# A cleared spare tile behind some gathers, and eleven row buffers for layer 1, in a two-layer graph network on Trainium2

## The chip, the cores and the metric

The kernel runs on one core of a Trainium2 chip. The metric is the device time of one execution in microseconds; the median of several executions counts. TensorE is PE in the profile (PEld is its weight load), VectorE is DVE, ScalarE is ACT, GpSimd is POOL, and SyncE (SP) issues most plain transfers. GpSimd issues all gathers, which are indirect DMA instructions: 128 row numbers go in, and 128 rows of a table in DRAM come out, one row to a partition.

## The reference

12,500 nodes with 128 features each and 200,000 edges, sorted by their destination. Everything is float32. Cut to what matters:

```python
h0 = maximum(layernorm(x), 0)
deg, wsum = segment_sum(1, dst), segment_sum(w, dst)
w = w / maximum(wsum, 1e-12)[dst]
feat = relu(h0 @ W_pool + b_pool)
neigh = segment_max(feat[src] * w, dst)          # layer 1: max over edges, 0 where deg is 0
rst = h0 @ W1_self + neigh @ W1_neigh + b1
h = relu(rst / maximum(norm(rst), 1e-12))
neigh2 = segment_sum(h[src] * w, dst) / maximum(deg, 1)   # layer 2: sum over edges
out = x + relu(h @ W2_self + neigh2 @ W2_neigh + b2)
```

Each layer fetches one row for every edge (`feat[src]`, `h[src]`), which is a gather of 200,000 rows of 512 bytes. That is done in groups.

## The kernel before, in words

**Groups.** The edges stand in 391 groups of 512 (the last has 320). A group's rows are fetched by four gathers of 128 rows, all issued by GpSimd in `gather` (L508, the instruction at L513). The nodes stand in 25 groups of four tiles of 128.

**Preparation.** The node groups are read, normalized and multiplied by W_pool: DVE takes the statistics, ACT makes the normalized tile (L622), PE transposes it (L624), ACT copies it out of PSUM (L645), PE multiplies it by W_pool (L647 for the bias, then L649, four matmuls that the trace shows as eight), and DVE or ACT clips the product at zero (`clip`, L608 for DVE), which goes to a table `feat_d` in DRAM. Background work on the edges (weights, degrees, flags) runs beside it on all engines. The table is complete only at the end of this stage. So that GpSimd isn't idle meanwhile, the first 17 edge groups (FIRST) gather rows of x itself, 68 gathers (called at L666); layer 1 normalizes and multiplies those edges' rows by W_pool itself (lines L527 to L557). GpSimd is kept in step with the preparation in its first part by a clear of a single column (L626), which waits for ACT.

**Layer 1.** Groups 17 to 390 gather rows of `feat_d` (called at L945). The consumer of a group is a pipeline over several steps: PE transposes the rows (L964), DVE multiplies by the weights (L1006), scans along the edges for a running maximum per destination (L979), picks and copies (L990, L999, L1002), PE transposes back (L1019), ACT copies (`rows`, L974), PE puts the rows at their nodes (L1028), and ACT adds that window to the layer's result (L914). Node groups whose edges are done are normalized and go to a table `h_d`.

**Layer 2.** Three early groups, and then groups 3 to 390, gather rows of `h_d` (called at L1127). DVE makes a matrix of places and weights (L1063, L1068), PE multiplies (L1075), and DVE adds the window (L1080). Node quads then make the output.

**Row buffers.** `buffer(g, wide)` says where group g's rows go. In layer 1 there is a ring of 18 buffers at first, then one of 14, and from group 113 on one of 4 (DEEP): memory that was lent is then in use for other things. The pool of full buffers itself has 11 tiles (RING + MORE). Layer 2 uses 4. The first gather of a group waits until PE has read what its buffer held; every gather also waits for the DMA of the gather eight before it. So the size of the ring is how many groups GpSimd can run ahead of the consumer.

**Order.** It is written out by hand in both layers and the preparation (manual schedules): each engine takes its instructions in the order of the code, and waits at the first whose inputs are not there.

Of the kernel before, what the change touches and what calls it, by code (L numbers as in the profile page):

```python
# [7 lines left out]
F32 = mybir.dt.float32  # L8
# [5 lines left out]
OP = mybir.AluOpType  # L14
# [4 lines left out]
P = 128  # L19
D = 128  # L20
# [16 lines left out]
LESS = 3 * WIDE  # L37
MID = 14
LEAST = LESS + 4 * MID
# [5 lines left out]
SCRATCH = 8192  # L45
MORE = 3
DEEP = 4


@with_exitstack  # L50
def gnn_kernel(ctx, tc, x, src, dst, ew, w_pool, b_pool, w1s, w1n, b1, w2s, w2n, b2, out):
# [13 lines left out]
    nc = tc.nc  # L65
# [6 lines left out]
    NG = GF + 1  # L72
# [4 lines left out]
    const = ctx.enter_context(tc.tile_pool(name="const", bufs=1))  # L77
    dram = ctx.enter_context(tc.tile_pool(name="dram", bufs=1, space=DRAM))

    feat_d = dram.tile([NP, D], F32, name="feat_d")  # L80
    h_d = dram.tile([NP, D], F32, name="h_d")
# [13 lines left out]
    bases = const.tile([1, NT * P], I32)  # L95
    unfit = const.tile([1, 1], I32)
    W = {name: const.tile([P, D], F32, name=f"w_{name}") for name in ("pool", "1s", "1n", "2s", "2n")}
    bp_all, b1_all, b2_all = (const.tile([P, D], F32, name=f"b_{i}") for i in range(3))
    ident = const.tile([P, P], F32)
    cols = const.tile([P, 2, LW], F32)  # L100

    both = ExitStack()
# [30 lines left out]
    def buffer(g, wide):  # L133
        if not wide:
            return full[g % DEEP]
        if WIDE <= g < WIDE + 3:
            k = g - WIDE
            return (work(f"f{k}").rearrange("p (q d) -> p q d", d=D) if k < 2 else ewT[:, 1])
        h = g if g < WIDE else g - 3
        if h < LESS:  # L140
            return ring[h % WIDE]
        return mid[(h - LESS) % MID] if h < LEAST else full[(h - LEAST) % DEEP]


    dr = rp.tile([P, NT, G + 2], I32)
# [63 lines left out]
    def load_rest():  # L209
# [11 lines left out]
        for t in range(1, NT):  # L221
# [3 lines left out]
            load_edges(nc.sync, ew, er, 0, t)  # L225


    diff = wk.tile([P, P], F32, bufs=1)
    nc.gpsimd.iota(diff, pattern=[[1, P]], base=0, channel_multiplier=-1,
                   allow_small_or_imprecise_dtypes=True)  # L230
    nc.gpsimd.iota(cols[:, 0, :], pattern=[[1, LW]], base=0, channel_multiplier=0,
                   allow_small_or_imprecise_dtypes=True)
# [3 lines left out]
    nc.gpsimd.iota(need, pattern=[[P, NT]], base=-LAG, channel_multiplier=1,  # L236
                   allow_small_or_imprecise_dtypes=True)
    nc.gpsimd.memset(agg1[:, NP:], 0.0)
    nc.vector.tensor_scalar(ident, diff, 0.0, None, op0=OP.is_equal)
    shift = {}  # L240
    for name, at in (("up", 1), ("up_wrap", 1 - P), ("down", -1), ("down_wrap", P - 1)):
        shift[name] = rp.tile([P, P], F32, name=f"shift_{name}")
        nc.vector.tensor_scalar(shift[name], diff, float(at), None, op0=OP.is_equal)
    nc.vector.tensor_scalar(need, need, RHO, None, op0=OP.mult)
    late_nodes = rp.tile([P, LATE], F32)
    nc.gpsimd.iota(late_nodes, pattern=[[P, LATE]], base=(HI - LATE) * P, channel_multiplier=1,
# [258 lines left out]
        ne = G if g < GF else TAIL  # L505
        return *divmod(g, P), ne, [(j, min(P, ne - j * P)) for j in range(-(-ne // P))]

    def gather(gt, table_d, g, only=None, last=None):  # L508

        t, r, ne, chunks = edges_of(g)  # L510
        limit = {} if last is None else dict(bounds_check=last, oob_is_err=False)
        for j, k in chunks if only is None else chunks[only:only + 1]:
            nc.gpsimd.indirect_dma_start(  # L513
                out=gt[:k, j, :], out_offset=None, in_=table_d[:, :],
                in_offset=bass.IndirectOffsetOnAxis(ap=srcT[:k, t, j, r:r + 1], axis=0), **limit)
        return gt


    gts = {}
# [43 lines left out]
    rest = load_rest()  # L563
# [47 lines left out]
    for i in range(len(groups) + 3):  # L611
# [50 lines left out]
        while raw_chunks and 1 <= i <= 17:  # L662
            r, j = raw_chunks[0]
            if r >= WIDE - NT and i < 15 or r > WIDE - 3 and i < 17 or i < 9 and len(raw_chunks) <= Q * FIRST - 3 * i:
                break
            gts[r] = gather(buffer(r, True), x, r, only=j)  # L666
            raw_chunks.pop(0)
        if i == len(groups) - 1:
            w_first, kt_first = (rp.tile([P, G], F32, name=f"r_f{k}") for k in range(2))
# [201 lines left out]
    with tc.manual_schedule(), tc.tile_pool(name="ew", bufs=3) as wk, \  # L871
# [61 lines left out]
        for i in range(max(turn) + 6):  # L933
# [8 lines left out]
            if i % KEPT == 0 and i and i + 2 < NG:  # L942
                keep_rows(i + 2, keep_tile())
            if FIRST <= i < NG:
                gts[i] = gather(buffer(i, True), feat_d, i)  # L945

            if i + 1 < NG:
                weight_rows(i + 1, wk.tile([P, G], F32, name="gs", bufs=2))
# [95 lines left out]
        i = NG  # L1044
# [5 lines left out]
    with tc.manual_schedule(), tc.tile_pool(name="ew2", bufs=3) as wk, \  # L1050
# [73 lines left out]
        first_groups = early_groups()  # L1124
        for i in range(max(turn) + 2):
            if EARLY <= i < NG:
                gts[i] = gather(buffer(i, False), h_d, i)  # L1127
                places(i)
            if EARLY <= i < NG:
                weighted(i)  # L1130
            if i + 4 in turn:
                n = turn[i + 4]
                if n % wide2(n) == 0:
                    xr = x_rows(wk, n, wide2(n), 2)
                xrs[n] = xr
            if late is not None:
                stages(late)
                late = None
            quad_stage(1)
            quad_stage(3)  # L1140
            if i in turn:
                n, xr = turn[i], xrs.pop(turn[i])
                if wide2(n) < Q:
                    late = nodes2(wk, ps, n, 1, strided(agg2, n, 1), xr)
                    next(late)
                elif n % Q == 0:
                    st = quad2(wk, pn, n, xr)
                    next(st)
                    for k in (1, 2, 3):
                        quads[i + k, k] = st  # L1150
            g = i - 1
            if EARLY <= g < NG:
                window_product(g)
            quad_stage(2)
            if i >= EARLY and i % 2:
                next(first_groups, None)
            if i == NG - 1:
                for n in (HI - 2, HI - 1):
                    own[n] = flip[:, 0] if n % 2 else ps.tile([P, Q, D], F32, name="pl", bufs=1)[:, 0]
                    linear_own(own[n], n, "2s")  # L1160
            g = i - 2
            if EARLY <= g < NG:
                window_add(g, window_at(mybir.EngineType.DVE, g))
# [122 lines left out]
```

## Time and profile before

| what | us |
|---|---|
| median of three runs | 4587.56 |
| the three runs | 4581.83, 4587.56, 4592.94 |
| the profiled execution, its own time | 4582.98 |
| its span, first to last instruction | 4581.2 |
| busy: POOL / PE / DVE / PEld / ACT | 2963.4 / 1950.3 / 1759.1 / 1623.2 / 422.1 |
| first and last gather of x | 10.60 and 110.91 |
| first and last gather of feat_d | 162.66 and 2347.16 |
| first and last gather of h_d | 2357.17 and 4568.24 |

The gathers' times are their starts on GpSimd. The span differs from the execution's own time by 1.8 us of start and end. In a row of a timeline, the number in brackets is the idle time of that engine before the instruction, with what ended it: another instruction, "issue" (nothing that the profile shows), or "remote" (in the chain of waits: "another core or an unknown queue"), a release whose origin the trace does not hold. In a row of windows stand the window, its length, and for each engine the busy time with the count of instructions, then the granted clock of PE, the share of the DMA engines and GB/s; where the view is limited to one line, only the engines that run that line have a column.

### The profile page before, as it was taken

Reading aid. Unit: us, or ns where it says so; the run is one execution under the profiler, and the core shown is the slowest. Engines: PE = TensorE matmul, PEld = TensorE weight load, DVE = VectorE, ACT = ScalarE, POOL = GpSimd, SP = SyncE. Lnnn points to the kernel's source line nnn. Section 1 sums busy time; section 2 is a strip of 40 time slices with the busy share of each in tenths; the row PEclk is TensorE's granted clock in tenths of the full one; section 3 lists DMA queues with packets and bytes.
Section 4 is the critical chain, followed back from the end, with each engine's and each line's share of the span. In section 5 each row is a group of like instructions: output and inputs, shape, how many; then the busy total and the mean of one; then the engine's idle time right before and its main releaser. Section 6 shows DMA issues by size and latency. Waiting matters only on the chain.

```text
span 4581.2 us, 30093 instructions
## 1 busy us (share of the span) xinstructions
PE 1950.3 (43%) x8086; PEld 1623.2 (35%) x8086; DVE 1759.1 (38%) x4405; ACT 422.1 (9%) x1257; POOL 2963.4 (65%) x3143
## 2 busy tenths in 40 slices
PE   3554444444344444443444443333333333333333
PEld 2443334333333333332344433333333333333333
DVE  3676667666666666665561111111111111111111
ACT  3531111111111111111110000000000000000000
POOL 5366664666666666666666666666666666666665
PEclk7765555555555555555555555555555555555555
DMA  4344444444444444443431122211121112112111
GB/s 134 107 117 122 127 120 117 117 119 120 117 119 117 117 120 118 118 121 113 120 96 48 46 57 55 54 51 51 50 56 51 51 51 55 52 51 56 51 51 51
DMA packets 193262, 396.94 MB, mean 87 GB/s; under 512 B 60623, under 2 KB 63822, under 8 KB 193088
## 3 DMA queue, kind: packets, MB, share of 16 engines
q0 software_dynamic: 100032, 204.97, 17.3%
q1 hardware_dynamic: 92320, 189.06, 13.6%
q8 instruction: 69, 1.13, 0.1%
q10 hardware_dynamic: 736, 0.92, 0.1%
q14 instruction: 105, 0.86, 0.1%
HBM read 374.96 MB, written 19.77 MB: 86 GB/s over the span
## 4 chain that ended last, share of the span: by engine, by line
POOL 29%; issue 26%; another core or an unknown queue 19%; DVE 13%; PE 11%; ACT 2%; DMA 1%; POOLq 0%; ACTq 0%; DVEq 0%
POOL gt L513 28%; DVE pm L979 4%; PE pm L964 3%; PE pn L1028 2%; DVE pm L1006 2%; PE two_pr L1019 2%; DVE sc L999 1%; DVE sq L816 1%; DVE sc L1002 1%; DMA gt<-h_d,srcT 1%; PE pa L1075 1%; PE pf L649 1%; ACT rows L974 1%; DVE sel L990 0%
## 5 line engine op out<-in xcount | busy, mean ns | idle before, releaser
L513 POOL DMA_INDIRECT gt<-h_d,srcT x1551 | 1467.7, 946 | 728.9 <-issue 414.2
L513 POOL DMA_INDIRECT gt<-feat_d,srcT x1303 | 1234.9, 948 | 671.8 <-issue 360.7
L1075 PE MATMUL pa<-s,gt 128*128 128x24 f32 x3102 | 716.7, 383 | 1260.4 <-DMA gt<-h_d,srcT 803.5
L1075 PEld LDWEIGHTS pa<-s,gt 128*128 128x128 f32 x3102 | 687.4, 325 | 1328.0 <-issue 813.2
L1080 DVE TENSOR_TENSOR way<-pa,way 128x41 f32 x391 | 77.7, 199 | 1726.2 <-remote 1016.0
L1019 PE MATMUL two_pr<-ident,sc 128*128 128x128 f32 x782 | 243.9, 412 | 942.4 <-ACT rows L974 557.2
L1006 DVE TENSOR_TENSOR pm<-pm,gs 128x512 f32<-128x512 f32 x390 | 271.8, 697 | 680.7 <-remote 428.4
L979 DVE TENSOR_TENSOR_SCAN pm<-kt,pm 128x512 f32<-128x512 bf16 x389 | 499.0, 1283 | 7.1
L1019 PEld LDWEIGHTS two_pr<-ident,sc 128*128 128x128 f32 x782 | 124.9, 201 | 1055.3 <-ACT rows L974 596.0
L964 PE MATMUL pm<-ident,gt 128*128 128x128 f32 x1303 | 323.8, 397 | 99.5 <-issue 54.3
L1028 PEld LDWEIGHTS pn<-sel,rows 128*128 128x128 f32 x1564 | 350.2, 308 | 0.2
L1028 PE MATMUL pn<-sel,rows 128*128 128x48 f32 x1564 | 334.7, 359 | 0.0
L964 PEld LDWEIGHTS pm<-ident,gt 128*128 128x128 f32 x1303 | 243.0, 222 | 135.3 <-issue 87.8
L974 ACT ACTIVATE rows<-two_pr 128x256 f32<-128x256 f32 x392 | 150.4, 384 | 1515.1 <-remote 1046.2
L990 DVE TENSOR_SCALAR sel<-cols,lastT,invT 128x48 f32<-128x48 f32 x782 | 253.4, 324 | 0.0
L832 ACT ACTIVATE oT<-pn,b_col 128x512 f32<-128x512 f32 x24 | 16.5, 689 | 2181.5 <-PE pn L797 701.8
L999 DVE COPY sc<-pm 128x256 f32<-128x256 f32 x391 | 165.8, 424 | 78.8 <-remote 67.3
L1002 DVE COPY_PREDICATED sc<-kt,pm 128x256 f32<-128x256 int16 x389 | 169.3, 435 | 3.9 <-remote 3.9
L513 POOL DMA_INDIRECT w2T<-feat_d,srcT x100 | 94.7, 947 | 97.8 <-DVE raw_mv L527 50.8
L1068 DVE TENSOR_TENSOR s<-place,w2T 128x96 f32<-128x96 f32 x391 | 100.8, 258 | 74.9 <-remote 35.0
L1063 DVE TENSOR_TENSOR place<-place,locT 128x96 f32<-128x96 f32 x391 | 100.9, 258 | 0.3 <-DVE way L1080 0.3
L914 ACT ACTIVATE way<-pn 128x48 f32 x391 | 81.8, 209 | 120.8 <-issue 46.9
(288 smaller groups left out, 1622.8 us busy)
## 6 DMA issues: line engine op xcount, KB each, us to landing
gs<-in_edge_weight SPq DMA_DIRECT2D x389, 256.0 KB
kt<-keep_d SPq DMA_DIRECT2D x97, 512.0 KB
gt<-h_d,srcT POOLq DMA_INDIRECT x1551
gt<-feat_d,srcT POOLq DMA_INDIRECT x1303
feat_d<-fr SPq DMA_DIRECT2D x24, 256.0 KB
xr<-in_x SPq DMA_DIRECT2D x24, 256.0 KB
out<-o SPq DMA_DIRECT2D x24, 256.0 KB
h_d<-sq SPq DMA_DIRECT2D x23, 256.0 KB
```

The lines of the kernel that those rows point to most:

```text
L513: nc.gpsimd.indirect_dma_start(out=gt[:k, j, :], out_offset=None, in_=table_d[:, :], in_offset=bass.IndirectOffsetOnAxis(ap=srcT[:k, t, j, ...
L964: nc.tensor.transpose(pms[i][:, j * P:j * P + k], gt[:k, j, :], ident[:k, :k])
L974: nc.scalar.activation(rws[g][:k, j, :], pr[:k, j, :], AF.Copy)
L979: nc.vector.tensor_tensor_scan(pm[:, :ne], kt[:, :ne], pm[:, :ne], carry, op0=OP.add, op1=OP.max)
L990: nc.vector.tensor_scalar(part, cols[:k, 1, :], lastT[:k, t, j, r:r + 1], invT[:k, t, j, r:r + 1], op0=OP.is_equal, op1=OP.mult)
L999: nc.vector.tensor_copy(sc[:, :ne // 2], two[:, :, 1])
L1002: nc.vector.copy_predicated(sc[:, :ne // 2], new[:, :, 1], two[:, :, 0])
L1006: nc.vector.tensor_tensor(pms[i][:, :n], rows[:, :n], ws.pop(i)[:, :n], OP.mult)
L1019: nc.tensor.transpose(prs[g][:k, j, :], sc[:, j * P:j * P + k], ident)
L1028: nc.tensor.matmul(pas[g], rows[:k, j, :], sel[:k, j, :], start=j == 0, stop=j == len(chunks) - 1)
L1063: nc.vector.tensor_tensor(hit, iota, locT[:, t, :, r:r + 1].to_broadcast([P, Q, PART]), OP.is_equal)
L1075: nc.tensor.matmul(pas[g][:, PART_AT[j]:PART_AT[j] + PART], gt[:k, j, :], s[:k, j, :], start=j == len(chunks) - 1, stop=j == 0, skip_group ...
```

## The change

Four things:

- `gather` has a new argument `rest`. With it, each gather instruction is followed on GpSimd by a `memset` of a tile `spare`, 128 partitions by 256 float32 columns, which nothing reads afterwards. It is set for the gathers of x except group 0's (64 instructions), for layer 1's groups up to 63 that gather `feat_d` (17 to 63, 188 instructions), for layer 1's last 26 groups (103) and layer 2's last 8 (31): 386 in all.
- In layer 1 the last ring has eleven buffers and not four; layer 2 keeps four.
- `spare` takes the memory of the bias row `bp_all`, which is read at the very start. The first clear waits for DVE to have read it; each further clear waits only for the clear before.
- To make room, the identity and the four shifted identities are slices of one 128x384 tile, made by one comparison in place of five.

```diff
+REST = 256
+REST_TO = 64
+REST_FROM = 26
+REST_END = 8
...
-    bp_all, b1_all, b2_all = (const.tile([P, D], F32, name=f"b_{i}") for i in range(3))
-    ident = const.tile([P, P], F32)
+    b1_all, b2_all = (const.tile([P, D], F32, name=f"b_{i}") for i in range(2))
+    spare = const.tile([P, REST], F32)
+    bp_all = spare[:, :D]
+    near_ones = const.tile([P, 3 * P], F32)
+    ident = near_ones[:, P:2 * P]
...
-        return mid[(h - LESS) % MID] if h < LEAST else full[(h - LEAST) % DEEP]
+        return mid[(h - LESS) % MID] if h < LEAST else full[(h - LEAST) % len(full)]
...
-    diff = wk.tile([P, P], F32, bufs=1)
-    nc.gpsimd.iota(diff, pattern=[[1, P]], base=0, channel_multiplier=-1,
+    diff = wk.tile([P, 3 * P], F32, bufs=1)
+    nc.gpsimd.iota(diff, pattern=[[1, 3 * P]], base=-P, channel_multiplier=-1,
...
-    nc.vector.tensor_scalar(ident, diff, 0.0, None, op0=OP.is_equal)
-    shift = {}
-    for name, at in (("up", 1), ("up_wrap", 1 - P), ("down", -1), ("down_wrap", P - 1)):
-        shift[name] = rp.tile([P, P], F32, name=f"shift_{name}")
-        nc.vector.tensor_scalar(shift[name], diff, float(at), None, op0=OP.is_equal)
+    nc.vector.tensor_scalar(near_ones, diff, 0.0, None, op0=OP.is_equal)
+    shift = {name: near_ones[:, P - at:2 * P - at]
+             for name, at in (("up", 1), ("up_wrap", 1 - P), ("down", -1), ("down_wrap", P - 1))}
...
-    def gather(gt, table_d, g, only=None, last=None):
+    def gather(gt, table_d, g, only=None, last=None, rest=False):
...
                 in_offset=bass.IndirectOffsetOnAxis(ap=srcT[:k, t, j, r:r + 1], axis=0), **limit)
+            if rest:
+                nc.gpsimd.memset(spare, 0.0)
...
-            gts[r] = gather(buffer(r, True), x, r, only=j)
+            gts[r] = gather(buffer(r, True), x, r, only=j, rest=r > 0)
...
-                gts[i] = gather(buffer(i, True), feat_d, i)
+                gts[i] = gather(buffer(i, True), feat_d, i, rest=i < REST_TO or i >= NG - REST_FROM)
...
-                gts[i] = gather(buffer(i, False), h_d, i)
+                gts[i] = gather(buffer(i, False), h_d, i, rest=i >= NG - REST_END)
```

On GpSimd in the gathers of x (groups 2 and 3; `gt_100` and the like are row buffers, `in_x` is x, `srcT` the row numbers, `way_65` the one-column clear of L626, DMASW the semaphores of earlier gathers). Before:

```order
L513 DMA gt_100<-in_x,srcT 128x128 [waits DMASW0_49]
L626 MEMSET way_65 128x1 [waits Activation_49]
L513 DMA gt_100<-in_x,srcT 128x128 [waits DMASW1_49]
L513 DMA gt_100<-in_x,srcT 128x128 [waits DMASW2_49]
L513 DMA gt_100<-in_x,srcT 128x128 [waits DMASW3_49]
L626 MEMSET way_65 128x1 [waits DMAHW0_49,Activation_49]
L513 DMA gt_101<-in_x,srcT 128x128 [waits DMASW4_49]
L513 DMA gt_101<-in_x,srcT 128x128 [waits DMASW5_49]
L513 DMA gt_101<-in_x,srcT 128x128 [waits DMASW6_49]
```

Now:

```order
L518 DMA gt_100<-in_x,srcT 128x128 [waits DMASW0_49]
L522 MEMSET spare 128x256 [waits Pool_49]
L633 MEMSET way_65 128x1 [waits Activation_49]
L518 DMA gt_100<-in_x,srcT 128x128 [waits DMASW1_49]
L522 MEMSET spare 128x256 [waits Pool_49]
L518 DMA gt_100<-in_x,srcT 128x128 [waits DMASW2_49]
L522 MEMSET spare 128x256 [waits Pool_49]
L518 DMA gt_100<-in_x,srcT 128x128 [waits DMASW3_49]
L522 MEMSET spare 128x256 [waits Pool_49]
L633 MEMSET way_65 128x1 [waits DMAHW0_49,Activation_49]
L518 DMA gt_101<-in_x,srcT 128x128 [waits DMASW4_49]
L522 MEMSET spare 128x256 [waits Pool_49]
```

Each gather of x is now followed by a clear that waits only for the clear before it (`Pool_49`); the order of the gathers and their own waits are the same.

On GpSimd at the end of layer 1, the rows of three groups among the last (`feat_d` is the table, PE is waited for at the first gather of a group, when its buffer is taken again). Before:

```order
L513 DMA gt_98<-feat_d,srcT 128x128 [waits DMASW6_49]
L513 DMA gt_98<-feat_d,srcT 128x128 [waits DMASW7_49]
L513 DMA gt_99<-feat_d,srcT 128x128 [waits DMASW0_49,PE_49]
L513 DMA gt_99<-feat_d,srcT 128x128 [waits DMASW1_49]
L513 DMA gt_99<-feat_d,srcT 128x128 [waits DMASW2_49]
L513 DMA gt_99<-feat_d,srcT 128x128 [waits DMASW3_49]
L513 DMA gt_100<-feat_d,srcT 128x128 [waits DMASW4_49,PE_49]
L513 DMA gt_100<-feat_d,srcT 128x128 [waits DMASW5_49]
L513 DMA gt_100<-feat_d,srcT 128x128 [waits DMASW6_49]
L513 DMA gt_100<-feat_d,srcT 128x128 [waits DMASW7_49]
```

Now:

```order
L518 DMA gt_106<-feat_d,srcT 128x128 [waits DMASW7_49]
L522 MEMSET spare 128x256 [waits Pool_49]
L518 DMA gt_107<-feat_d,srcT 128x128 [waits DMASW0_49,PE_49]
L522 MEMSET spare 128x256 [waits Pool_49]
L518 DMA gt_107<-feat_d,srcT 128x128 [waits DMASW1_49]
L522 MEMSET spare 128x256 [waits Pool_49]
L518 DMA gt_107<-feat_d,srcT 128x128 [waits DMASW2_49]
L522 MEMSET spare 128x256 [waits Pool_49]
L518 DMA gt_107<-feat_d,srcT 128x128 [waits DMASW3_49]
L522 MEMSET spare 128x256 [waits Pool_49]
L518 DMA gt_108<-feat_d,srcT 128x128 [waits DMASW4_49,PE_49]
L522 MEMSET spare 128x256 [waits Pool_49]
```

Before, the ring is `gt_98` to `gt_101`; now it goes on to `gt_108`, so that the wait for PE is for the group eleven back, and a clear follows each gather.

On GpSimd in layer 2, where its last eight groups begin (the table is `h_d`), now:

```order
L518 DMA gt_100<-h_d,srcT 128x128 [waits DMASW3_49,PE_49]
L518 DMA gt_100<-h_d,srcT 128x128 [waits DMASW4_49]
L518 DMA gt_100<-h_d,srcT 128x128 [waits DMASW5_49]
L518 DMA gt_100<-h_d,srcT 128x128 [waits DMASW6_49]
L518 DMA gt_101<-h_d,srcT 128x128 [waits DMASW7_49,PE_49]
L522 MEMSET spare 128x256 [waits Pool_49]
L518 DMA gt_101<-h_d,srcT 128x128 [waits DMASW0_49]
L522 MEMSET spare 128x256 [waits Pool_49]
L518 DMA gt_101<-h_d,srcT 128x128 [waits DMASW1_49]
L522 MEMSET spare 128x256 [waits Pool_49]
L518 DMA gt_101<-h_d,srcT 128x128 [waits DMASW2_49]
L522 MEMSET spare 128x256 [waits Pool_49]
```

Up to that group nothing has changed in layer 2; from it on a clear stands behind each gather. The orders of PE, ACT and SP are the same as before apart from names, and DVE has four instructions fewer at the start.

## The prediction, made before the changed kernel had run

> **What bounds the kernel now.** I read the page's chain first, then the waits of the span, then single stages by windows.
>
> ```profile
> POOL 29%; issue 26%; another core or an unknown queue 19%; DVE 13%; PE 11%; ACT 2%; DMA 1%; POOLq 0%; ACTq 0%; DVEq 0%
> L513 POOL DMA_INDIRECT gt<-h_d,srcT x1551 | 1467.7, 946 | 728.9 <-issue 414.2
> L513 POOL DMA_INDIRECT gt<-feat_d,srcT x1303 | 1234.9, 948 | 671.8 <-issue 360.7
> ACT rows L974 <- remote: 1046.2, 116, 19.2
> POOL gt L513 <- issue: 783.3, 2562, 1.9
> POOL gt L513 <- remote: 441.9, 158, 5.7
> DVE pm L1006 <- remote: 428.4, 82, 10.3
> POOL gt L513 <- PE pm L964: 96.8, 36, 37.3
> ```
>
> The chain is the gathers (POOL with its "issue", 55%) and then a releaser that the profile cannot name: 19% "another core or an unknown queue", in the list of waits "remote". There is one core here, so it is something inside it. A wait row reads: total, times, longest. POOL, ACT and DVE all wait for it. What it looks like in time, in layer 2 (start, duration, instruction, idle before it):
>
> ```profile
> 3014.38 0.95 POOL L513 DMA_INDIRECT gt<-h_d,srcT  x1 [0.30 <-issue]
> 3020.05 0.20 DVE L1080 TENSOR_TENSOR way<-pa,way 128x41 f32 x1 [15.43 <-remote]
> 3020.29 0.95 POOL L513 DMA_INDIRECT gt<-h_d,srcT  x1 [4.96 <-remote]
> ```
>
> DVE stood still for 15.43 us, POOL ran on for ten of them until it too had to wait, and 4.7 us after POOL's last gather had ended (3015.33) both went on within 0.25 us. I read that as PE's results being reported late while gathers follow each other closely, and reported at once when POOL pauses. The test is a stage where POOL is idle and one where it isn't. PE's main product of the preparation (L649, 8 matmuls a node group), PE busy with its count first:
>
> ```profile
> 47.00:106.00 59.00, 4.37 (x16) 3.88 (x16) 0.54 0.21 57
> 106.00:158.00 52.00, 35.18 (x132) 31.62 (x132) 0.90 0.37 123
> ```
>
> With gathers of x running, 2 node groups in 59 us; with POOL idle, 16.5 in 52 us, 3.15 us each. The same for layer 1's multiplication (L1006, one a group):
>
> ```profile
> 283.00:430.00 147.00, 19.41 (x28) 0.55 0.43 121
> 753.00:785.00 32.00, 6.00 (x9) 0.66 0.38 114
> 850.00:2300.00 1450.00, 177.16 (x254) 0.56 0.42 118
> ```
>
> 5.25 us a group early, 5.71 in the long middle, but 3.56 in the 32 us in which POOL is idle (the 37.3 us of the waits, where its lead goes from 14 buffers to 4). So layer 1 is not limited by the four gathers of a group alone: these have a pitch of 1.25 us (0.95 and 0.30), 5.0 us a group. What is late is released by POOL's pauses. Layer 2 is limited by the gathers themselves with a stall now and then: 728.9 idle, of which 414.2 is the 0.30 of each.
>
> **The price of a clear.** Nothing of 128x256 runs on POOL before. The nearest rows:
>
> ```profile
> L626 POOL MEMSET way<- 128x1 f32 x7 | 0.8, 115 | 6.6 <-ACT xn L622 6.6
> L229 POOL IOTA diff<- 128x128 f32 x1 | 0.2, 233 | 0.4 <-POOLq L1267 0.4
> L236 POOL IOTA need<- 128x4 f32 x1 | 0.1, 130 | 0.0
> L238 POOL MEMSET way<- 128x48 f32 x1 | 0.1, 128 | 0.0
> 13.29 0.95 POOL L513 DMA_INDIRECT gt<-in_x,srcT  x1 [0.30 <-issue]
> 14.23 0.12 POOL L626 MEMSET way<- 128x1 f32 x1
> 14.55 0.94 POOL L513 DMA_INDIRECT gt<-in_x,srcT  x1 [0.19 <-issue]
> ```
>
> A clear of one column starts where the gather ends, and the next gather starts 0.20 us after it: it lies wholly in the 0.30. By the memsets' own slope, (128 - 115) / 47 = 0.28 ns a column, 256 columns take 0.19 us; by the iotas', (233 - 130) / 124 = 0.83 ns, 0.33 us. With 0.20 behind it the pitch becomes 0.95 + 0.19 + 0.20 = 1.34 to 1.48 us, so a clear costs POOL 0.09 to 0.23 us. Nothing is the lowest end (if it overlaps the next gather's start too). I take 0.20, since the iota of 128 columns is the row nearest in size: pitch 1.45, 5.8 us a group.
>
> The Trainium skill (GPSIMD Engine Reference, Elementwise — side-by-side cycle accounting) gives a body of about 1.03 cycles a column at 1.2 GHz, which for 256 columns is an estimate of 0.22 us beside a fixed cost; the iota rows' slope agrees with it and the memsets' does not. With it the pitch would be at the upper end, and the sum below would stay.
>
> **The change part by part.** Only the 386 clears and the eleven buffers count. The wider iota and the single comparison in place of five run before the first gather waits for ACT (10.60 us), so they are covered.
>
> What a clear may give: POOL's pause between two gathers (0.30 now) becomes 0.39 to 0.53 us in which it writes a tile and starts no transfer. Whether that lets the late reports through, no row shows. Bounds: nothing, since a one-column clear behind every third gather did not end the stall from 21.39 to 31.83 us below (one of them stands in it, at 25.50); all, since an idle POOL does. I take half, as an estimate, and call it the share. What it is a share of:
>
> ```profile
> 25.50 0.11 POOL L626 MEMSET way<- 128x1 f32 x1
> 21.39 10.44 another core or an unknown queue
> 45.98 18.97 another core or an unknown queue
> 67.30 8.85 another core or an unknown queue
> 79.29 23.70 issue
> 192.40 7.53 another core or an unknown queue
> 201.18 4.36 another core or an unknown queue
> 206.57 13.67 another core or an unknown queue
> 96.10 0.94 POOL L513 DMA_INDIRECT w2T<-in_x,srcT  x1 [0.30 <-issue]
> 162.66 0.95 POOL L513 DMA_INDIRECT w2T<-feat_d,srcT  x1 [50.81 <-DVE raw_mv L527]
> ```
>
> (1) 64 clears in the gathers of x. The chain of the preparation loses 10.44 + 18.97 + 8.85 + 23.70 = 62 us to the late reports (the "issue" piece lies in the same gap: PE has no work in it). Half is **-31 us**. The clears themselves, 64 x 0.2 = 13 us, lie on POOL, which afterwards waits 50.8 us anyway. Bounds: +13 (no relief; the starved stretch lasts as long as the gathers, which now end later) to -48 (60 gathers later by 12 us end at 109, four more at 1.45 end near 115, and before that the first gather of feat_d can't start: 162.66 - 115).
>
> (2) 188 clears, layer 1's groups 17 to 63. While POOL issues these, the consumer works on groups 0 to about 45. The part up to group 17 loses 7.53 + 4.36 + 13.67 = 25.6 us to late reports: half, **-13** (0 to -26). Groups 17 to 45: 28 groups, 5.25 - 3.56 = 1.69 us each above the unstarved pace, half of it is **-24** (0 to -47). POOL pays 188 x 0.2 = 38 us; it has them:
>
> ```profile
> 166.00:283.00 117.00, 74.09 (x80) 0.65 0.36 100
> 283.00:430.00 147.00, 94.67 (x100) 0.55 0.43 121
> ```
>
> 180 gathers at 1.25 us are 225 of 264 us, so 39 us are stalls for a free buffer. With that cover gone the consumer meets POOL with a lead shorter by the 68 us it has gained, some 12 groups, and POOL then runs without pauses until the lead stands at 14 again. In that time the consumer is slower. From 5.0 us of running and 0.71 us of pause a group, with 0.71 / 3.56 = 0.2 group done in the pause, 0.8 is left for 5.0 us: 6.25 us a group unpaused. Twelve groups of lead at (1/5.0 - 1/6.25) a us take 300 us, and cost 300 x 0.54 / 6.25 = 26; less, since the lead above 14 was to be given up anyway: **+20** (0 to +38).
>
> (3) Eleven buffers for four from group 113 on. The idle 37.3 us at 785 shrink to about 3 groups of 3.56, since the lead goes from 14 to 11 only; the fast stretch there loses about 7 groups x (5.71 - 3.56) = 15 us. The same 7 groups are found again at the end, where POOL stops with eleven in flight, and not four. **0** (-5 to +5).
>
> (4) 103 clears behind the last 26 groups. POOL takes 26 x 5.8 = 151 us for them, against 148 at the present pace. Without relief the consumer does 26.4 of the last 37 groups meanwhile and 10.6 at 3.56, 189 us. With half, 5.71 - 1.08 = 4.63 us: 32.6 in 151 us, 4.4 at 3.56, 167. **-20** (+2 to -38, the last with all of it and a consumer at POOL's heels: 151 us).
>
> ```profile
> 2347.16 0.91 POOL L513 DMA_INDIRECT gt<-feat_d,srcT  x1 [0.31 <-issue]
> 2357.17 1.03 POOL L513 DMA_INDIRECT er<-h_d,srcT  x1 [9.10 <-DVE pm L1006]
> 4568.24 0.91 POOL L513 DMA_INDIRECT gt<-h_d,srcT  x1 [0.30 <-issue]
> ```
>
> That end is seen in POOL's 9.10 us wait for DVE before the first gather of h_d.
>
> (5) 31 clears at the end of layer 2. Here POOL sets the end (from the last gather at 4568.24 it is 13 us to 4581.2), so 31 x 0.2 = +6; a stall like the 4.96 us one above may fall out. **+3** (-2 to +7).
>
> Sum: -31 - 13 - 24 + 20 + 0 - 20 + 3 = -65 us. The profiled execution took 4582.98 us, span 4581.2; that gives 4518. The median of the three runs is 4587.56, 4.6 above, so **4523 us**.
>
> **A rule that speaks against it.** Beside the lateness there is another way in which a clear could reach DVE. The Trainium skill (SBUF — State Buffer, SBUF: two separate sides) says that VectorE and GpSimd share a port pair which one instruction holds for its whole length, so a clear could block a DVE instruction that needs it. No run here shows it; by the rows 291 clears of layer 1 x 0.33 us x DVE's busy share there (900.68 of 1450 us) is 60 us, the last rival below.
>
> ```profile
> 850.00:2300.00 1450.00, 636.09 (x2763) 510.33 (x2764) 900.68 (x1747) 180.12 (x602) 960.66 (x1014) 0.56 0.42 118
> ```
>
> **The rivals.**
> A. The share is half: 4523; with a share of 0.3 to 0.7 about 4490 to 4560.
> B. Nearly all late reports come through: -48 - 26 - 47 + 38 - 38 - 2 = -123, **4465**. For it: 3.15 and 3.56 us a group once POOL is idle. Against it: the gather's 0.95 us stays, and what a report needs may be a longer pause; it took 4.7 us of idle at 3020.
> C. A clear overlaps the 0.30 us and changes nothing: 4588, no change, for (3) alone is 0. For it: the one-column clear that moved no gather.
> D. Slower: a clear costs POOL its 0.2 us and frees no report. The place is the preparation, where PE stays starved until POOL has ended, +13; the end of layer 1 +2, of layer 2 +6: +21, **4609**. It decides when a report needs over half a microsecond of quiet. For it: the stall at 21.39 with clears of one column running. In groups 17 to 63 the 38 us go into POOL's stalls.
> E. Clears hold DVE up: +60 on top of D, about **4670**.
>
> **How the numbers follow.** A 0.56, B 0.13, C 0.12, D 0.15, E 0.04. This kernel's three runs lie 11 us apart, so 0.2% (9 us) is about what can be told from no change. Faster is A and B, 0.69; same is C, 0.12; slower D and E, 0.19. The range reaches from just under B (4460) to nearly D (4605); A's own is 4490 to 4560.
>
> **What would show it.** Pitch of gathers with a clear 1.34 to 1.48, clears 190 to 330 ns. More than 2 node groups of L649 in 47 to 106 us, the first gather of feat_d at about 130 in place of 162.66 (D: 170 or later). Groups 17 to 45 at about 4.4 us in place of 5.25. The longest wait of a gather for pm falls from 37.3 to about 11 us. The middle stays at 5.71 us a group and layer 2 at its length of 2211 us from the first gather of h_d to the last. If the preparation does not shorten, the step "half" is wrong; if the middle or layer 2 moves, something else is at work.

## The result, and the profile after

The changed kernel took 4523.77 us (median of four runs, 4519.46 to 4540.04), the kernel before 4584.69 us in the same comparison: a ratio of 0.9871, 95% interval 0.9843 to 0.9900. The forecast was 4523.

The profiled execution is the slowest of the four (4540.04, span 4538.2), so its difference to the profile before is only 43 us, where the medians differ by 61. I therefore also use the profile of a second measurement of the same kernel (4521.27, span 4519.5), called "changed, second profile" below. From the page of the first, the chain by engine, the gathers of `feat_d` and the clears:

```profile
POOL 27%; issue 25%; another core or an unknown queue 20%; DVE 12%; PE 12%; ACT 2%; DMA 1%; POOLq 0%; ACTq 0%; SPq 0%; DVEq 0%
L518 POOL DMA_INDIRECT gt<-feat_d,srcT x1303 | 1236.0, 949 | 587.3 <-issue 334.7
L522 POOL MEMSET spare<- 128x256 f32 x386 | 127.2, 330 | 0.3
```

The picture as a whole has not changed: the shares of the chain are within two points of those before, and the nameless release still has a fifth of it. What has changed stands in a few stretches: GpSimd's idle time before the gathers of `feat_d` falls from 671.8 to 587.3 us, and a clear takes 330 ns. On GpSimd's timeline of the second profile, the first gather with a clear behind it and the next:

```profile
15.82 0.95 POOL L518 DMA_INDIRECT gt<-in_x,srcT  x1 [0.30 <-issue]
16.76 0.34 POOL L522 MEMSET spare<- 128x256 f32 x1
17.26 0.95 POOL L518 DMA_INDIRECT gt<-in_x,srcT  x1 [0.16 <-issue]
```

From 15.82 to 17.26 is 1.44 us; without a clear it is 1.25. The preparation, in the first of the two windows that the prediction showed (PE's product by W_pool, now line 656), and two rows of the list of waits, all of the first profile:

```profile
47.00:106.00 59.00, 24.29 (x88) 21.37 (x88) 0.66 0.39 116
POOL w2T L518 <- DVE raw_mv L534: 23.9, 1, 23.9
POOL gt L518 <- PE pm L971: 56.1, 35, 21.8
```

With the gathers of x running, 11 node groups are multiplied in 59 us, where it was 2. GpSimd's wait for the end of the preparation falls from 50.8 to 23.9 us, and its longest wait for a free buffer from 37.3 to 21.8 us.

To see where the 43 and the 62 us come from, I cut the span where layer 1's multiplication by the weights starts on the same group in each kernel (L1006, now L1013). The six windows of each kernel hold 17, 28, 55, 20, 230 and 39 groups: first the groups whose rows of x were gathered early, then groups up to about 45 (while GpSimd issues the gathers with clears), up to 100, the change of the ring near 113, the long middle, and the last 39. The start of the first window is the length of the preparation; columns are the window, its length, DVE's busy time on that line with the count, then clock, DMA share and GB/s. Before:

```profile
170.56:292.08 121.52, 11.88 (x17) 0.64 0.36 99
292.08:444.23 152.15, 19.54 (x28) 0.54 0.42 119
444.23:731.95 287.72, 38.32 (x55) 0.58 0.44 126
731.95:830.56 98.61, 13.95 (x20) 0.57 0.39 115
830.56:2141.66 1311.10, 160.41 (x230) 0.57 0.43 119
2141.66:2356.59 214.93, 27.23 (x39) 0.56 0.40 114
```

Changed, first profile:

```profile
141.19:235.88 94.69, 11.86 (x17) 0.59 0.40 115
235.88:360.84 124.96, 19.55 (x28) 0.57 0.49 137
360.84:691.18 330.34, 38.30 (x55) 0.56 0.41 116
691.18:812.75 121.57, 13.92 (x20) 0.58 0.38 108
812.75:2128.65 1315.90, 160.14 (x230) 0.56 0.42 118
2128.65:2310.74 182.09, 27.22 (x39) 0.57 0.44 128
```

Changed, second profile:

```profile
138.45:229.52 91.07, 11.85 (x17) 0.69 0.40 117
229.52:353.34 123.82, 19.56 (x28) 0.58 0.50 138
353.34:692.86 339.52, 38.34 (x55) 0.55 0.40 114
692.86:806.07 113.21, 13.93 (x20) 0.56 0.39 114
806.07:2122.26 1316.19, 160.19 (x230) 0.56 0.42 118
2122.26:2291.46 169.20, 27.16 (x39) 0.56 0.46 134
```

Read down the lengths: the preparation is 29 and 32 us shorter, the first 17 groups 27 and 30, the next 28 groups 27 and 28. The next 55 groups then take 43 and 52 us more, the change of the ring 23 and 15 more, the middle 5 more, and the last 39 groups 33 and 46 less. From the last multiplication to the end it is 2224.6 us before (4581.2 - 2356.6) and 2227.5 and 2228.0 now. The two profiles of the same kernel differ by 13 us in the last window and by 9 and 8 in the third and at the ring, and so much one profile can be off.

The 43 and 52 us of the third window are lost right after the clears stop (the last one starts at 407.33 us in the first profile and at 404.82 in the second). GpSimd's gathers from there on and layer 1's multiplications in the same 81 us, both in the second profile, and then the multiplications in the first:

```profile
405.00:486.00 81.00, 61.19 (x64) 0.52 0.32 88
405.00:486.00 81.00, 3.81 (x6) 0.52 0.32 88
405.00:486.00 81.00, 5.29 (x8) 0.56 0.32 88
```

64 gathers in 81 us are 1.27 us each, so GpSimd hardly pauses in the second profile; and the consumer does six groups, 13.5 us each. In the first it does eight, 10.1 us each.

### The profile page after: what moved, and what is told of

Read it like the earlier page. It is cut to its first block, busy times and chain, and to the rows that moved or that the text cites. A ratio compares the mean times of both kernels' runs of the same rounds, so it can differ in the third digit from the quotient of the medians.

```text
span 4538.2 us, 30474 instructions
## 1 busy us (share of the span) xinstructions
PE 1958.0 (43%) x8086; PEld 1623.8 (36%) x8086; DVE 1761.6 (39%) x4401; ACT 421.4 (9%) x1257; POOL 3091.6 (68%) x3529
## 4 chain that ended last, share of the span: by engine, by line
POOL 27%; issue 25%; another core or an unknown queue 20%; DVE 12%; PE 12%; ACT 2%; DMA 1%; POOLq 0%; ACTq 0%; SPq 0%; DVEq 0%
POOL gt L518 26%; DVE pm L986 4%; PE pm L971 3%; PE pn L1035 3%; PE two_pr L1026 2%; DVE pm L1013 2%; DVE sq L823 2%; DVE sc L1006 1%; DMA gt<-h_d,srcT 1%; DVE sc L1009 1%; PE pa L1082 1%; PE pf L656 1%; ACT rows L981 1%; DVE sel L997 0%
## 5 line engine op out<-in xcount | busy, mean ns | idle before, releaser
L518 POOL DMA_INDIRECT gt<-feat_d,srcT x1303 | 1236.0, 949 | 587.3 <-issue 334.7
L1026 PE MATMUL two_pr<-near_ones,sc 128*128 128x128 f32 x782 | 243.9, 412 | 956.1 <-ACT rows L981 555.0
L1013 DVE TENSOR_TENSOR pm<-pm,gs 128x512 f32<-128x512 f32 x390 | 271.5, 696 | 691.0 <-remote 438.6
L1026 PEld LDWEIGHTS two_pr<-near_ones,sc 128*128 128x128 f32 x782 | 123.7, 200 | 1070.3 <-ACT rows L981 600.0
L971 PE MATMUL pm<-near_ones,gt 128*128 128x128 f32 x1303 | 324.1, 398 | 81.2 <-issue 50.3
L971 PEld LDWEIGHTS pm<-near_ones,gt 128*128 128x128 f32 x1303 | 244.4, 223 | 116.6 <-issue 76.2
L1006 DVE COPY sc<-pm 128x256 f32<-128x256 f32 x391 | 165.4, 423 | 64.8 <-remote 38.6
L518 POOL DMA_INDIRECT w2T<-feat_d,srcT x100 | 95.7, 957 | 59.3 <-DVE raw_mv L534 23.9
L522 POOL MEMSET spare<- 128x256 f32 x386 | 127.2, 330 | 0.3
```

Source lines behind the costliest of these rows:

```text
L518: nc.gpsimd.indirect_dma_start(out=gt[:k, j, :], out_offset=None, in_=table_d[:, :], in_offset=bass.IndirectOffsetOnAxis(ap=srcT[:k, t, j, ...
L522: nc.gpsimd.memset(spare, 0.0)
L971: nc.tensor.transpose(pms[i][:, j * P:j * P + k], gt[:k, j, :], ident[:k, :k])
L1006: nc.vector.tensor_copy(sc[:, :ne // 2], two[:, :, 1])
L1013: nc.vector.tensor_tensor(pms[i][:, :n], rows[:, :n], ws.pop(i)[:, :n], OP.mult)
L1026: nc.tensor.transpose(prs[g][:k, j, :], sc[:, j * P:j * P + k], ident)
```

## The experiments

The theory on record was: PE's reports come late while gathers follow closely, a clear makes a pause of half a microsecond, and through that pause part of them comes. Rivals: any instruction between two gathers does it; the eleven buffers make the gain; it is the write of a whole tile that matters and not the pause.

One thing has to be said first, since without it the numbers can't be understood: the four sets of runs below differ in the very thing that is studied. The kernel before, run beside each set, takes 3952.73 us in the first, 4587.57 in the second (4584.69 in the comparison above), 4622.98 in the third and 3952.70 in the fourth. With the sets the record gives the chip numbers 4, 12, 15 and 15. So number 15 stands beside 4623 us and, 16 minutes later, beside 3953: whether the chip makes the difference, the machine, or something that changes with time, is not shown. Below, a set is one in which reports are late or one in which nothing is late.

### First set: nothing is late

```diff
 # clears in the gathers of x alone, four buffers
-        ... feat_d, i, rest=i < REST_TO or i >= NG - REST_FROM)
+        ... feat_d, i, rest=False)
-        ... h_d, i, rest=i >= NG - REST_END)
+        ... h_d, i, rest=False)
-        ... else full[(h - LEAST) % len(full)]
+        ... else full[(h - LEAST) % DEEP]
```

> Clears behind the 64 gathers of x alone; four buffers as before. Theory (a pause of about half a microsecond on POOL lets PE's late reports through): the first gather of feat_d stands near 133 us as in the changed kernel, in place of 162.66, and 10 to 30 us of it reach the end: 4555 to 4575. Rival (the eleven buffers make the gain): 4580 to 4590, first gather of feat_d near 133 all the same. Rival (the clears in the gathers of x make the whole gain): 4520 to 4530.

```diff
 # eleven buffers, no clear
-        ... x, r, only=j, rest=r > 0)
+        ... x, r, only=j, rest=False)
         # and rest=False for feat_d and h_d
```

> Eleven buffers in layer 1, no clear at all. Theory: what is lost at 785 us, where the lead no longer falls to four, is found again at the end of layer 1: 4580 to 4590, with layer 1's last part about 20 us shorter and the stretch at 753 to 785 us about 15 to 23 us longer. Rival (the buffers make the gain): 4520 to 4545.

```diff
 # clears of one column
-                nc.gpsimd.memset(spare, 0.0)
+                nc.gpsimd.memset(spare[:, 0:1], 0.0)
```

> All 386 clears write one column in place of 256; eleven buffers. A clear of one column lies in the 0.30 us between gathers, so the pitch stays at 1.25 us. Theory (the length of the pause counts): hardly a report comes through, the first gather of feat_d stands at 155 to 165 us, total 4575 to 4590. Rival (any instruction of POOL between two gathers does it): the first gather of feat_d near 133 us, total 4515 to 4530.

```diff
 # all clears, four buffers
-        ... else full[(h - LEAST) % len(full)]
+        ... else full[(h - LEAST) % DEEP]
```

> All clears as in the changed kernel, four buffers as before from group 113 on. Theory: the gain up to group 100 (41 us in the profile of the changed kernel) stays, since the fast stretch of the falling lead comes back, but the end of layer 1 gains nothing, for its clears find a lead of four only: 4540 to 4555. Rival (the buffers make the gain): 4575 to 4590. Rival (the buffers do nothing even with the clears): 4520 to 4530.

Measured, against 3952.73 us for the kernel before: x alone 3956.08 (ratio 1.001, 1.000 to 1.002), eleven buffers alone 3953.18 (1.0005, 0.9995 to 1.0014), clears of one column 3953.44 (1.0006, 0.9997 to 1.0016), all clears with four buffers 4019.06 (1.0173, 1.0156 to 1.0190). None of the expected totals could be met, for the kernel before is 632 us faster here with the same gathers. The list of waits of the run with eleven buffers and no clear has no "remote" at all; the releasers have names:

```profile
ACT rows L981 <- PE pn L1035: 1165.4, 344, 7.9
DVE pm L1013 <- PE pm L971: 420.9, 216, 5.0
```

The windows by groups of the same run (no clear), of which the first, second, third, fifth and sixth are shown, and then the third and sixth of the run with all clears and four buffers:

```profile
107.47:195.56 88.09, 11.85 (x17) 0.67 0.41 125
195.56:295.90 100.34, 19.41 (x28) 0.62 0.57 167
295.90:532.31 236.41, 38.29 (x55) 0.58 0.53 151
...
631.53:1784.93 1153.40, 160.53 (x230) 0.56 0.48 134
1784.93:1977.48 192.55, 27.23 (x39) 0.54 0.47 133
```

```profile
299.99:576.57 276.58, 38.38 (x55) 0.55 0.47 134
1832.10:2044.22 212.12, 27.25 (x39) 0.53 0.42 121
```

The middle runs at 1153.4 / 230 = 5.01 us a group, four gathers of 1.25: here GpSimd alone sets the pace. The preparation is over at 107 and not at 171 us. The engines' work is the same (GpSimd is busy for 2959.0 us in this run and 2963.4 in the profile before, DVE for 1771.6 and 1759.1). So I read this set as what the kernel would be with no late report, and put the 4585 - 3953 = 632 us of the comparison above down to the late reports. The set shows also what the clears cost where there is nothing to free: 276.58 - 236.41 = 40 us for the 188 clears of layer 1's first groups and 19.6 us for the 103 of the last. The total is 66 us. The four against the eleven buffers make no difference here.

### Second set: the changed kernel, clears twice, x alone, one column

Reports are late here, and the kernel before took 4587.57 us.

> The changed kernel itself beside the kernel before. If the kernel before takes about 4585 us here, the reports of PE come late here as in its first profile: the change takes about 4524 (ratio 0.987), and this second profile shows which of the terms the first one, at 4540, had smaller than the other runs. If the kernel before takes about 3953 us, as in the first four experiments, nothing waits for a late report: theory (a clear frees late reports and costs POOL 0.2 us), nothing to free, 386 clears to pay, of which those in the gathers of x lie partly beside other work: 4010 to 4030, ratio 1.015 to 1.02. Rival (the clears help by something else, so also here): ratio under 1.

```diff
 # each clear twice
                 nc.gpsimd.memset(spare, 0.0)
+                nc.gpsimd.memset(spare, 0.0)
```

> Each clear is done twice in a row, so that POOL's pause between two gathers grows by a further 0.33 us or more. Where reports are late, theory (the length of the pause counts): more of them come through in the preparation, first gather of feat_d at 115 to 133 us, but layer 1's first groups now cost POOL about 7.2 us each and bound it: 4530 to 4600. Rival (any instruction does it): first gather of feat_d as with one clear, and the total longer by what POOL pays. Where reports are not late: longer than with one clear by 250 to 322 clears of about 0.35 us, 4100 to 4140.

> Clears behind the 64 gathers of x alone, four buffers, once more. Where reports are late, theory: first gather of feat_d near 133 us, 10 to 30 us of these 29 reach the end, 4555 to 4575. Rival (the clears of layer 1 and the eleven buffers carry nothing): 4520 to 4530. Where they are not late: 3956 again.

> All 386 clears write one column, so that the pitch of the gathers stays at 1.25 us. Where reports are late, theory (the length of the pause counts): first gather of feat_d at 155 to 165 us, total 4575 to 4590. Rival (any instruction of POOL between two gathers does it): first gather of feat_d near 133 us, total 4515 to 4530. Where they are not late: 3953 again.

Measured: the changed kernel 4522.91 (ratio 0.9862, 0.9846 to 0.9879), two clears 4657.48 (1.0151, 1.0134 to 1.0168), x alone 4555.05 (0.9932, 0.9915 to 0.9948), one column 4602.63 (1.0036, 1.0025 to 1.0048).

**x alone** (64 clears) gives 32.5 us, half of the whole gain, at the theory's lower end; the first gather of `feat_d` starts at 131.06 us. Its first three windows:

```profile
139.07:260.66 121.59, 11.87 (x17) 0.64 0.36 99
260.66:412.80 152.14, 19.49 (x28) 0.57 0.42 119
412.80:700.20 287.40, 38.29 (x55) 0.59 0.43 126
```

The preparation ends 31.5 us earlier, and every later stretch, the three that aren't shown too, is as before to within 4 us. So these 32 us reach the end whole; and the 27 us in each of the next two windows of the changed kernel, and the 43 to 52 us that it loses after them, both belong to the 188 clears.

**One column**: the pitch stays at 1.25 us and nothing is freed; the total is 13 us above the theory's 4590. The first, fourth and last window:

```profile
175.60:298.35 122.75, 11.86 (x17) 0.58 0.36 98
...
738.53:857.55 119.02, 13.93 (x20) 0.56 0.38 109
...
2172.48:2376.62 204.14, 27.15 (x39) 0.59 0.39 115
```

So it isn't that any instruction between two gathers would do. Since these clears do nothing, the run also shows what the eleven buffers do by themselves where reports are late: 20 us more near group 113, 11 us less at the end, about 10 us lost. (GpSimd then stands 40.24 us at the end of layer 1 waiting for the consumer; it stood 9.10 before.) The buffers don't make the gain.

**Two clears**: the first three windows.

```profile
110.23:202.45 92.22, 11.87 (x17) 0.60 0.36 106
202.45:361.57 159.12, 19.54 (x28) 0.54 0.38 108
361.57:771.35 409.78, 38.35 (x55) 0.55 0.35 99
```

The preparation is now over at 110 us, as in the runs in which nothing is late (107 to 112): two clears free all of its 60 us, one clear half of them. (The first gather of `feat_d` starts only at 134.58, since the gathers of x now last until then.) But two clears cost GpSimd 0.55 us (a median pitch of 1.80 us), it needs 7.2 us a group, and the groups behind pay for it: the third window takes 122 us more than before, and the total is 57 us above the theory's 4600. Two clears between two gathers free more than one; the price decides. Since two clears are a longer pause and also twice the writing, the run doesn't tell which of them frees the reports.

### Third set: the end alone, and one partition

Reports are late here too, and the kernel before took 4622.98 us.

```diff
 # clears of layer 1's last 26 groups alone, eleven buffers
-        ... x, r, only=j, rest=r > 0)
+        ... x, r, only=j, rest=False)
-        ... feat_d, i, rest=i < REST_TO or i >= NG - REST_FROM)
+        ... feat_d, i, rest=i >= NG - REST_FROM)
         # and rest=False for h_d
```

> Eleven buffers and the clears behind the last 26 groups of layer 1 alone: none in the gathers of x, in groups 17 to 63 and in layer 2. Where the kernel before takes about 4585 us: theory (the clears at the end let the consumer run at 3.6 to 4.6 us a group, and the eleven buffers pay for them) layer 1's last 39 groups take about 170 to 182 us as in the changed kernel (215 before), the buffers give away 15 to 20 us near group 113 as the run with clears of one column shows: total 4555 to 4575. Rival (the end's gain is that of the buffers alone): as the run without these clears, near 4600. Where the kernel before takes about 3953 us: 103 clears to pay, 3970 to 3980.

```diff
 # clears of one partition
-                nc.gpsimd.memset(spare, 0.0)
+                nc.gpsimd.memset(spare[0:1, :], 0.0)
```

> All 386 clears as in the changed kernel, but each writes one partition of the 128, so that it lasts about as long and writes 1/128 of the bytes. Where the kernel before takes about 4585 us: theory (the pause between two gathers counts) 4515 to 4535, first gather of feat_d at 128 to 136 us. Rival (what counts is the write of a whole tile, or the use of all of GpSimd's lanes) first gather of feat_d at 155 to 170 us, 4575 to 4605. Where the kernel before takes about 3953 us: both say 4015 to 4025, and the run tells only the price of a clear.

Measured: the end alone 4613.39 (0.9975, 0.9960 to 0.9989), one partition 4616.24 (0.9978, 0.9968 to 0.9989). The base is 35 us higher here than the expectations have it, so they are to be read as ratios: the end alone is at the upper edge of what the theory expected (0.993 to 0.998), and its last 39 groups take longer than the 170 to 182 us expected; one partition is far from the theory's 0.985 to 0.989 and at the edge of the rival's 0.998 to 1.004. The first two and the last window of the end alone, then the first two and the last of one partition, and GpSimd's timeline of the latter:

```profile
170.78:295.39 124.61, 11.86 (x17) 0.61 0.36 97
295.39:445.13 149.74, 19.53 (x28) 0.56 0.42 120
...
2190.11:2382.21 192.10, 27.20 (x39) 0.55 0.41 120
```

```profile
163.72:279.95 116.23, 11.87 (x17) 0.60 0.36 100
279.95:428.25 148.30, 19.54 (x28) 0.55 0.43 123
...
2173.27:2374.50 201.23, 27.22 (x39) 0.56 0.39 115
15.88 0.94 POOL L518 DMA_INDIRECT gt<-in_x,srcT  x1 [0.30 <-issue]
16.81 0.30 POOL L522 MEMSET spare<- 1x256 f32 x1
17.27 0.95 POOL L518 DMA_INDIRECT gt<-in_x,srcT  x1 [0.16 <-issue]
```

This is the result that my theory did not foresee. A clear of one partition makes nearly the same pause (1.39 us from gather to gather in these rows, against 1.44; the medians over the gathers of x are 1.41 and 1.45), but, beside the end alone, whose preparation has no clears, it frees 7 us of the preparation where whole clears free 29 to 32, 8 us of the first 17 groups where they free 27 to 30, and 1 us of the next 28. Length of the pause is not enough, then, unless the last 0.04 us of it count for more than all the rest, or reports respond more weakly to whole clears too in this set. The end alone points that last way a little: with whole clears its last 39 groups take 192 us, 9 us less than with one partition, while they took 169 to 182 in the changed kernel.

### Fourth set: both kinds of clear in one kernel, and clears in the middle

The first of these was to have both kinds of clear in one set.

```diff
 # one partition in groups 17 to 63, whole clears elsewhere, four buffers
-                nc.gpsimd.memset(spare, 0.0)
+                nc.gpsimd.memset(spare if rest == 1 else spare[0:1, :], 0.0)
-        ... feat_d, i, rest=i < REST_TO or i >= NG - REST_FROM)
+        ... feat_d, i, rest=2 if i < REST_TO else int(i >= NG - REST_FROM))
-        ... else full[(h - LEAST) % len(full)]
+        ... else full[(h - LEAST) % DEEP]
```

> The run with clears of one partition was on another chip than the runs of the changed kernel, so here both kinds stand in one kernel: whole clears in the gathers of x and in the last 26 groups of layer 1, clears of one partition behind the gathers of groups 17 to 63; and four buffers from group 113 on. Where the kernel before takes 4585 us or more: if the write of the whole tile is what counts, the first gather of feat_d stands at 128 to 136 us, but groups 17 to 45 take 140 to 152 us as before, not 123 to 125 as in the changed kernel; if the pause counts, they take 120 to 130. With four buffers, groups 100 to 120 take about 99 us as before (115 to 122 with eleven), and the last 39 groups, whose clears now find a lead of four, 200 us or more against 170 to 182. Total 4550 to 4575; if the eleven buffers are of no use to the end, 4520 to 4540.

```diff
 # as changed, and a clear behind every second gather in the middle
-            if rest:
+            if rest == 1 or rest == 2 and j % 2:
-        ... feat_d, i, rest=i < REST_TO or i >= NG - REST_FROM)
+        ... feat_d, i, rest=1 if i < REST_TO or i >= NG - REST_FROM else 2)
```

> The changed kernel, and besides a whole clear behind every second gather in the middle of layer 1 (groups 64 to 364). Where the kernel before takes 4585 us or more: POOL's gathers alone would then take 5.38 us a group there in place of 5.0, and 5.71 is what a group takes now. If a clear frees reports so that POOL's stalls fall by more than the 0.38 us, the middle runs at 5.4 to 5.6 us a group and the total is 30 to 90 us under the changed kernel's; if the clears are only paid, 5.8 to 6.1 us a group and 30 to 110 us above it. Theory leans to the second, about 4550 to 4600: groups 17 to 63 with a clear behind each gather ran POOL at 5.85 us a group.

They ran where nothing is late (before: 3952.70), so neither question was answered. Both kinds: 4014.05 (1.0157, 1.0143 to 1.0171). Every second gather: 4136.78 (1.0467, 1.0452 to 1.0481). The second gives the price of a clear over many of them: it has 602 clears more than the first set's run with all clears and four buffers (the kernel before is the same there to 0.03 us), and takes 4136.78 - 4019.06 = 117.7 us more, 0.196 us each. Its middle runs at 1243.17 / 230 = 5.41 us a group:

```profile
698.64:1941.81 1243.17, 160.61 (x230) 0.55 0.44 125
```

## Why the prediction was right, point by point

The total was right to the microsecond, which is partly luck: several terms were off and balanced.

- **What bounds the kernel: right, as far as the traces go.** The prediction showed DVE and POOL going on at 3020.05 and 3020.29 us. PE's rows around that point, in the profile before, show that no matmul had just ended:

```profile
3012.00 1.87 PE L1075 MATMUL pa<-s,gt 128*128 128x24 f32 x8 [3.19 <-DMA gt<-h_d,srcT]
3020.82 1.87 PE L1075 MATMUL pa<-s,gt 128*128 128x24 f32 x8 [6.95 <-remote]
```

PE had been done since 3013.87, so what the others waited for was the report and not the work. And in the sets in which no wait has that name, the kernel takes 632 us less, and the middle of layer 1 runs at exactly four gathers a group.

- **The price of a clear, 0.20 us: right.** Pitch 1.44 us in the rows, 0.196 us over 602 clears. The clear takes 330 ns, the upper bound by the slope of the iotas; the slope of the one- and 48-column memsets was misleading. The Trainium skill (GPSIMD Engine Reference, Elementwise — side-by-side cycle accounting) gave an estimate of 0.22 us and a fixed cost; with the one-column clear's 0.12 us as that cost it comes to 0.34, and the trace agrees with 0.33.
- **The share, half: right for one clear in the preparation.** 29 and 32 us of the 60 that the reports cost there (171 against 107 to 112 us). In the first 17 groups it was too low: 27 and 30 us of 33 (121.5 against 88.1), where I had 13. In the next 28 groups 27 and 28 of 52, where I had 24.
- **Step 1, -31 us: right**, -29 and -32, and -31.5 with these clears alone, -32.5 in that run's time.
- **The refill, +20 us, was mis-sized**: 43 and 52 us, beyond its bound of 38. The mechanism was the one named (GpSimd makes up its lead without a pause, and the consumer is slow meanwhile), but the pace of the consumer without pauses was put at 6.25 us a group and is 10.1 and 13.5 in the 81 us after the clears. The consumer, 83 and 91 us ahead by group 45, is 41 and 39 ahead at group 100. With it, step 2 as a whole gave 11 and 6 us, where the sum had 17. The 188 clears bring little.
- **Step 3, eleven buffers at 0, was wrong in size**: about 10 us lost, by the run with one column. The fast stretch at 753 to 785 us was worth 20, and not 15, and the end gave back 11.
- **Step 4, -20 us at the end: right or too small**, which of them the profiles leave open: ring and end together are -10 and -31 us in the two profiles, and with the buffers' own 10 us of loss taken out the clears of the last 26 groups brought 20 to 41. The run with the end alone says 20: its time is 9.6 us under the kernel before, with the same buffers.
- **Step 5, +3 us: not told apart from nothing.** It is +3 in both profiles, but the same stretch is 2.7 us longer with clears of one column too, which cost nothing.
- **The middle** took 5 us more, and 4 in x alone and one column; no step had it, and it is within what these profiles differ by.
- **Rival D is what happens where nothing is late**: all clears with four buffers cost 66 us there, ratio 1.0173. It is more than the rival's 21, since GpSimd has no stalls there in which the 188 clears would be free. The changed kernel itself was not run in those sets. **Rival C** (the clear overlaps) is refuted by the pitch, **B** (nearly all reports come through) by the preparation, 29 and 32 us where it had 48, and by groups 17 to 45, 27 and 28 where it had 47. **Rival E** is not seen: DVE's copy (now L1006) and multiplication (L1013) take 423 and 696 ns on average, against 424 and 697 before, and in the window of 28 groups, with clears running, one multiplication takes 698 ns as before (19.55 / 28), so nothing shows of the lock that the Trainium skill (SBUF — State Buffer, SBUF: two separate sides) describes for two engines on one port pair.
- **The mechanism in my words, a pause, is open.** Two clears free more than one, and a clear of one column, which makes no pause, frees nothing (in the stall from 21.39 us that the prediction named, two of the kernel's own such clears stand, at 21.74 and 25.50, and not one); but one of nearly the same length on a single partition freed a quarter, in another set. That the write over all partitions matters is the simplest reading and not shown, since the run that would have settled it came where nothing is late. What makes the reports late in the first place is open as well.

Where reports are late, no run had a lower ratio to the kernel before than the changed kernel. By the terms above, its 64 clears in the gathers of x and the 103 at the end carry most of the gain; leaving out the other 219 wasn't tried.

## What to carry to other kernels

When consumers wait for a release that the profile can't name, and go on together shortly after the issuing engine has paused, look at what that engine does back to back, and compare a stage in which it is idle. A pause put there is only free where the engine has slack that the end doesn't see: here the same clear gave 32 us in the preparation, 6 to 11 us net in the next stage, where most of what it gave was lost as soon as it stopped, and nothing that could be told at the end of layer 2, where the producer sets the end. And measure such a change in more than one set of runs, on more than one chip: it gains 1.3% where reports come late, and clears of the same number cost 1.7% where they don't.

## What was not expected of the hardware

The kernel before took 3953, 4585 to 4588 and 4623 us in different sets of runs, with a gather pitch of 1.25 us wherever no clear makes it longer, and the granted clock alike (0.54 to 0.56 in its runs). Where it takes 3953 us, no wait in the traces has the name "remote". What makes PE's reports late in some sets stays open; it need not be the chip, for number 15 stands with both. And a clear's effect depends on how many partitions it writes, or seems to: 29 to 32 us of the preparation with 128 partitions, 7 with one, in different sets, at nearly the same length (330 and 303 ns).
